# A transformer block on one core: queries and keys by seven block products in place of eight, and the second FFN layer's weights read from DRAM

## The chip, the cores and the metric

The kernel runs on one NeuronCore of a Trainium2 chip. The core has five engines, each with its own queue of instructions, tied to each other by semaphores: TensorE (PE in the profile; its weight loads are a row of their own, PEld), VectorE (DVE), ScalarE (ACT), GpSimd (POOL) and SyncE (SP), which here only issues DMAs. Matmuls write to PSUM, everything else lives in SBUF. The metric is the time of one execution in microseconds. Before the change the median of three runs is 2196.39 us (2195.55 to 2197.65).

## The reference, cut to what matters

A parallel block: layer norm, then attention with rotary embedding and a three-layer FFN side by side, and both are added to x. There are 16 batches of 512 tokens with 256 features, 8 heads of 128, and FFN layers of 1024, 1024 and 256 whose weights are +1 or -1.

```python
xn = _layernorm(x)                                # x: (16, 512, 256) float32
q = rope(einsum('bim,mhd->bhid', xn, wq))
k = rope(einsum('bim,mhd->bhid', xn, wk))
v = einsum('bim,mhd->bhid', xn, wv)
s = einsum('bhid,bhjd->bhij', q, k) / 128 - 1e30 * (i < j)
p = softmax(s)
att = einsum('bhim,hdm->bim', einsum('bhij,bhjd->bhid', p, v), wo)
h = concatenate([xn, -xn])
for kb, s_i in ((k0, s0), (k1, s1), (k2, s2)):    # relu(h) * 2 between layers
    h = s_i * (h @ where(kb, 1.0, -1.0))
out = x + att + h
```

For one head q (128 by 512, features by tokens) is wq's two 128-row blocks times xn's two 128-feature blocks, and k is the same with wk.

## The kernel before, in words

**Slots.** The work is cut in slots, one for each head of each batch: 128 slots, g = 8 b + h. TensorE's order is written out by hand: all code from L580 on runs under a manual schedule for PE. The order on the other engines is chosen by the framework's scheduler, which takes a program's order as priority and puts an instruction where it thinks that its inputs are ready; `behind` (L198) adds an order without a semaphore. A plain slot (`slot`, L547, heads 2 to 7) issues on TensorE: the queries and keys of the next head (`project_qk(g + 1)`), score row 0 of its own head, `ffn2` of the tile two heads back (8 records of 256 columns), row 1, four matmuls of `ffn1`, row 2, four more, row 3, four more, the output projection of head g - 2 (`project_o`), the rest of the `ffn1` tile, and `attend(g - 1)`, the product of v with the transposed probabilities of the slot before. Slots of heads 2 and 7 end with `project_v` (6.9 us of matmuls). Head 0's slot (`slot_of_head_0`) holds the last tile of the batch before and the whole first FFN layer (`ffn0`); head 1's (`slot_of_head_1`) has no `ffn2`, and the output projection stands behind row 0. A matmul with float32 operands shows as two records, one with float32r operands as one.

**Queries and keys.** `project_qk` (L314) makes q and k by two 512-column matmuls each, into one PSUM bank each of a ring of three (`ps_mm`). ACT copies the two halves of the partitions crosswise into `sw` (L326, L327), DVE multiplies the PSUM tile by `cos_sb` (L329), GpSimd multiplies `sw` by `sin_sb` (L330) and adds (L331). The results are qT and kT, wanted by the score rows of the next slot. wq is scaled by 1/128 beforehand (`scale_wq`).

**Probabilities.** `score_row` (L335) is one matmul; DVE adds the causal mask and takes the maximum (L340, L342), ACT the exponential (L345), DVE the reciprocal of the sum, rl (L347), GpSimd the product (L348). Two PSUM banks hold the rows. `turn` (L352) transposes 32 by 32 blocks on DVE into z (L356), and `carry` (L233) moves them to their places in pT by sixteen small DMAs, 40 KB each, from SP's queue. `attend` in the next slot reads pT.

**FFN.** `ffn0` and `ffn1` (L424, L443) split each activation in a high and a low float32r part (ACT makes the high one, DVE the low one). The weights are made once from bytes: `make_w1` makes all of w1, 1024 by 1024, and it stays in SBUF (32 KB of each partition) for all batches.

**The next batch's xn.** `layernorm` (head 3), `transpose_xn` (head 4) and `carry_xn_out` (end of head 5) put it through DRAM; `carry_xn_back` (head 6, one DMA behind each score row, from ACT's queue) brings it to the layout xnT, from which `split_xn` (head 7) makes the FFN's inputs.

Of the kernel before, what the change touches and what calls it, by code (L numbers as in the profile page):

```python
# [11 lines left out]
U8 = mybir.dt.uint8  # L12
# [10 lines left out]
def kernel(  # L23
# [79 lines left out]
    x_first = xpool.tile([P, NT, M], F32, tag="x", name="x_first")  # L103
# [4 lines left out]
    wq_sb = wpool.tile([P, NM, HD], F32, tag="wq", name="wq_sb")  # L108
    wk_sb = wpool.tile([P, NM, HD], F32, tag="wk", name="wk_sb")
# [6 lines left out]

    cos_sb = cpool.tile([P, T], F32, tag="cos", name="cos_sb")
# [4 lines left out]
    k1_sb = work.tile([P, NF0, F1], U8, tag="v", name="k1_sb")  # L122
# [3 lines left out]
    load_w(nc.sync, wq_sb, wq, 0, 2)  # L126
    load_w(nc.scalar, wk_sb, wk, 0, 2)
# [8 lines left out]
    load_w(nc.sync, wq_sb, wq, 2, H)  # L136
    load_w(nc.sync, wk_sb, wk, 2, H)
    nc.sync.dma_start(k1_sb, k1.rearrange("(c p) f -> p c f", p=P))
# [14 lines left out]
    w1_sb = wpool.tile([P, NF0, F1], F32R, tag="w1", name="w1_sb")  # L153
# [26 lines left out]
    def make_w1(reduced, raised):  # L180
        for c in range(NF0):
            if c % 2:
                behind(nc.scalar.activation(
                    w1_sb[:, c, :], k1_sb[:, c, :], AF.Identity,
                    bias=nsg_sb[:, 1:2], scale=sg2_sb[:, 1:2],
                ), raised)
            else:
                behind(nc.vector.tensor_scalar(
                    w1_sb[:, c, :], k1_sb[:, c, :], sg2_sb[:, 1:2], sg_sb[:, 1:2],
                    ALU.mult, ALU.subtract,  # L190
                ), reduced)
# [14 lines left out]
    xns, zxs, bounces, xnTs, halves = {}, {}, {}, {}, {}  # L206

    def layernorm(b, xt, after=None):

        st = small.tile([P, NT, nc.vector.BN_STATS_DIM], F32, tag="st", name=f"st_{b}", bufs=2)  # L210
        mv = small.tile([P, NT, nc.vector.BN_AGGR_DIM], F32, tag="mv", name=f"mv_{b}", bufs=2)
        for c in range(NT):
            begun = nc.vector.bn_stats(st[:, c, :], xt[:, c, :])
            behind(begun, after)
            nc.vector.bn_aggr(mv[:, c, :], st[:, c, :])
        rs = small.tile([P, NT], F32, tag="rs", name=f"rs_{b}", bufs=2)
        nc.gpsimd.tensor_scalar(rs, mv[:, :, 1], LN_EPS, None, ALU.add)
        raised = nc.gpsimd.tensor_tensor(rs, rs, half_sb, ALU.pow)
        xn = npool.tile([P, NT, M], F32, tag="xn", name=f"xn_{b}")
        for c in range(NT):  # L220
            nc.vector.tensor_scalar(
                xn[:, c, :], xt[:, c, :], mv[:, c, 0:1], rs[:, c : c + 1],
                ALU.subtract, ALU.mult,
            )
        xns[b] = xn
        return raised
# [22 lines left out]
    def transpose_xn(b, after):  # L249
        xn = xns.pop(b)  # L250
        zx = work.tile([P, NQ, NM, NT, Q], F32, tag="z", name=f"zx_{b}")
        for c in range(NT):
            behind(nc.vector.transpose(
                zx[:, :, :, c, :].rearrange("p j m a -> p m j a"),
                xn[:, c, :].rearrange("p (m j a) -> p m j a", j=NQ, a=Q),
            ), after)
        zxs[b] = zx
# [36 lines left out]


# [18 lines left out]
    def project_qk(g):  # L314
        b, h = divmod(g, H)
        res = []
        for name, w in (("q", wq_sb), ("k", wk_sb)):
            pq = ps_mm.tile([P, T], F32, tag="mm", name=f"p{name}_{b}_{h}")
            for m in range(NM):
                nc.tensor.matmul(  # L320
                    pq, w[:, m, ts(h, D)], tokens(xnTs[b], m),
                    start=(m == 0), stop=(m == NM - 1),
                )

            sw = work.tile([P, T], F32, tag="sw", name=f"sw{name}_{b}_{h}")
            nc.scalar.copy(sw[0:HALF, :], pq[HALF:D, :])  # L326
            nc.scalar.copy(sw[HALF:D, :], pq[0:HALF, :])  # L327
            rt = work.tile([P, T], F32, tag=f"{name}T", name=f"{name}T_{b}_{h}")
            nc.vector.tensor_tensor(rt, pq, cos_sb, ALU.mult)  # L329
            nc.gpsimd.tensor_tensor(sw, sw, sin_sb, ALU.mult)  # L330
            nc.gpsimd.tensor_tensor(rt, rt, sw, ALU.add)  # L331
            res.append(rt)
        qks[g] = res
# [109 lines left out]
    def ffn1(b, f):  # L443
        ph = ps_mm.tile([P, T], F32, tag="mm", name=f"ph1_{b}_{f}")
        for c in range(NF0):
            for i in range(2):
                nc.tensor.matmul(  # L447
                    ph, w1_sb[:, c, ts(f, P)], h0s[b][i][:, c, :],
                    start=(c == 0 and i == 0), stop=(c == NF0 - 1 and i == 1),
                )  # L450
                if c < NF0 - 1 or i == 0:
                    yield
# [22 lines left out]
    def scale_wq(engine, h0, h1, after):  # L475

        for c in range(NM):
            cols = wq_sb[:, c, h0 * D : h1 * D]
            if engine is nc.scalar:
                behind(engine.mul(cols, cols, 1.0 / D), after)  # L480
            else:
                behind(engine.tensor_scalar(cols, cols, 1.0 / D, None, ALU.mult), after)

    def first_slot():
        l0 = [ffn0(0, f) for f in range(NF0)]
        project_qk(1)
        rest(project_v(0, 0))
        for ic in range(NT):
            reduced, raised = score_row(0, ic)
            rest(l0[ic])  # L490
        turn(0, reduced)
        scale_wq(nc.scalar, 2, H, raised)
        rest(*l0[NT:])
        make_w1(reduced, raised)

    def slot_of_head_0(g):

        b = g // H
        if b < B:
            l0 = [ffn0(b, f) for f in range(NF0)]  # L500
            project_qk(g + 1)
        last = ffn2(b - 1, NF1 - 1)
        if b == B:
# [4 lines left out]
            return  # L508
        for ic in range(NT):
            reduced, _ = score_row(g, ic)  # L510
            if ic == 0:
                rest(ffn2(b - 1, NF1 - 2))
            elif ic == 1:
                rest(ffn1(b - 1, NF1 - 1))
# [10 lines left out]
    def slot_of_head_1(g):  # L525
        b = g // H
        if b < B:
            project_qk(g + 1)
            tile = ffn1(b, 0)
        else:  # L530
            tile = iter(())
        for ic, n in enumerate((0, 4, 3, 3)):
            if b < B:
                reduced, _ = score_row(g, ic)
            if ic == 0 and g > 1:
                project_o(g - 2)
            some(tile, n)
        if g == 1:
            make_w2(reduced)
        if b < B:  # L540
# [6 lines left out]
    def slot(g):  # L547
        b, h = divmod(g, H)
        if g + 1 < N_SLOTS:
            project_qk(g + 1)  # L550
        tile = ffn1(b, h - 1)
        for ic in range(NT):
            reduced, raised = score_row(g, ic)
            if h == H - 2 and b + 1 < B:
                carry_xn_back(b + 1, ic, raised)
            if ic == 0:
                rest(ffn2(b, h - 2))
            else:
                some(tile, 4)
        turn(g, reduced)  # L560
# [4 lines left out]
        attend(g - 1)  # L565
        if h == 2:
            for gv in range(1, HD // (VH * D)):
                rest(project_v(b, gv))
        if b + 1 < B:
            if h == H - 3:  # L570
                carry_xn_out(b + 1, raised)
# [8 lines left out]
    with tc.manual_schedule(engines={mybir.EngineType.PE}):  # L580
        with tc.manual_schedule(engines={mybir.EngineType.DVE}):
            scale_wq(nc.gpsimd, 0, 2, layernorm(0, x_first))
            transpose_first_xn()
            make_scales()
            project_qk(0)
# [57 lines left out]
```

## Time and profile before

| | |
|---|---|
| median of three runs | 2196.39 us |
| the profiled execution | 2196.68 us, of which the span from first to last instruction is 2194.7 |
| granted TensorE clock | 0.999 of full speed |
| matmuls pq and pk (L320) | 512 + 512 records of 128x512 |
| DMA engines | mean 57 GB/s; pT<-z 2048 issues, 1.9 us to landing |
| HBM | 23.33 MB read, 16.25 MB written |

A row of a group of instructions reads: line, engine, operation, out<-in by the program's names, shape and count, busy time, mean duration of one, and the idle time of the engine just before them with what ended it. In a timeline the columns are start and duration in us, engine, line, operation, names and count, and in brackets the idle time before and its releaser. The ends of matmuls are modelled, so the step from one start to the next is what a matmul costs. From batch to batch it is 135.6 us (two slots of head 1 start at 990.25 and 1125.84).

### The profile page before, as it was taken

How to read it: one execution, taken by the hardware profiler on the slowest of the kernel's cores; microseconds unless marked ns; L12 is line 12 of the kernel's file. 1: busy time of each engine (PE TensorE's matmuls, PEld its weight loads, DVE VectorE, ACT ScalarE, POOL GpSimd, SP SyncE). 2: the span in 40 equal slices, each digit the busy share in tenths (PEclk: the TensorE clock that was granted, in tenths of full speed). 3: DMA queues.
4: the chain of work that ended last, by engine and by line, in shares of the span. 5: the costliest groups of instructions: out<-in, count | busy, mean ns of one | idle time of the engine just before them, and what ended most of it. 6: DMA issues, size and time to landing. Idle time of an engine off the chain costs nothing.

```text
span 2194.7 us, 30483 instructions
## 1 busy us (share of the span) xinstructions
PE 2168.8 (99%) x9736; PEld 1548.3 (71%) x9736; DVE 1191.9 (54%) x3005; ACT 867.3 (40%) x1945; POOL 944.6 (43%) x1067
## 2 busy tenths in 40 slices
PE   7999999999999999999999999999999999999998
PEld 3677777777777777776776767777777777777766
DVE  5545655456555565555655555555545655456544
ACT  5344343343434344343343433434334343443432
POOL 4443534435344353434534344353533534435342
PEclk9999999999999999999999999999999999999999
DMA  5122212222121221212211122121221211222111
GB/s 161 41 63 56 61 42 55 59 56 66 43 58 50 57 67 44 60 48 56 67 51 55 49 57 64 52 59 44 56 68 51 60 43 52 66 55 59 43 44 51
DMA packets 134286, 125.55 MB, mean 57 GB/s; under 512 B 37744, under 2 KB 130928, under 8 KB 134128
## 3 DMA queue, kind: packets, MB, share of 16 engines
q1 hardware_dynamic: 122192, 107.09, 18.5%
q10 hardware_dynamic: 11936, 16.52, 2.2%
q8 instruction: 78, 1.28, 0.2%
q14 instruction: 80, 0.66, 0.1%
HBM read 23.33 MB, written 16.25 MB: 18 GB/s over the span
## 4 chain that ended last, share of the span: by engine, by line
PE 97%; SPq 1%; DMA 1%; ACT 1%; DVE 0%; issue 0%; POOL 0%; ACTq 0%; DVEq 0%
PE ph L447 21%; PE y L399 15%; PE po L373 13%; PE s L339 12%; PE pv L307 10%; PE pq L320 10%; PE pk L320 10%; PE ph L432 5%; SPq L237 1%; DMA wk_sb<-in_L_attn_wk_dram 0%; DMA pT<-z 0%; DVE z L356 0%; DMA k_sb<-in_L_ffn_k_dram 0%; POOL swk L330 0%; POOL kT L331 0%
## 5 line engine op out<-in xcount | busy, mean ns | idle before, releaser
L330 POOL TENSOR_TENSOR swq<-swq,sin_sb 128x512 f32<-128x512 f32 x128 | 165.5, 1293 | 959.6 <-ACT swq L327 959.6
L447 PE MATMUL ph<-h0h,w_sb 128*128 128x512 f32 x1024 | 517.9, 506 | 0.0
L345 ACT ACTIVATE p<-s,nmax 128x128 f32<-128x128 f32 (+3 forms) x512 | 270.6, 529 | 380.3 <-DVE nmax L342 329.6
L447 PE MATMUL ph<-h0l,w_sb 128*128 128x512 f32 x1024 | 408.8, 399 | 0.0
L339 PE MATMUL s<-kT,qT 128*128 128x128 f32 (+3 forms) x1024 | 360.5, 434 | 1.9 <-ACT p L345 1.9
L348 POOL TENSOR_SCALAR p<-p,rl 128x128 f32<-128x128 f32 (+3 forms) x512 | 269.7, 537 | 203.9 <-DVE rl L347 202.5
L329 DVE TENSOR_TENSOR qT<-pq,cos_sb 128x512 f32<-128x512 f32 x128 | 88.6, 692 | 462.2 <-ACT swq L327 462.2
L373 PEld LDWEIGHTS po<-pT,v 128*128 128x128 f32 x2560 | 304.7, 192 | 17.4 <-issue 4.4
L373 PE MATMUL po<-pT,v 128*128 128x128 f32 x2560 | 306.9, 275 | 3.7 <-DMA pT<-z 3.1
L356 DVE STREAM_TRANSPOSE z<-p 128x128 f32<-128x128 f32 (+3 forms) x512 | 234.2, 489 | 70.5 <-POOL p L348 64.0
L342 DVE TENSOR_REDUCE nmax<-s 128x1 f32<-128x128 f32 (+3 forms) x512 | 251.4, 491 | 12.7
L339 PEld LDWEIGHTS s<-kT,qT 128*128 128x128 f32 x1024 | 183.6, 189 | 88.8 <-issue 60.8
L447 PEld LDWEIGHTS ph<-h0h,w_sb 128*128 128x128 f32 x1024 | 193.0, 188 | 73.6 <-issue 26.9
L447 PEld LDWEIGHTS ph<-h0l,w_sb 128*128 128x128 f32 x1024 | 193.2, 189 | 72.8 <-issue 26.9
L399 PE MATMUL y<-wo_sb,oT 128*128 128x256 f32 x1024 | 241.8, 379 | 0.8 <-DVE oT L379 0.8
L320 PE MATMUL pq<-xnT,wq_sb 128*128 128x512 f32 x512 | 241.8, 595 | 0.0
L320 PE MATMUL pk<-xnT,wk_sb 128*128 128x512 f32 x512 | 240.7, 592 | 0.5 <-DVE qT L329 0.5
L307 PE MATMUL pv<-wv_sb,xnT 128*128 128x512 f32 x512 | 227.0, 596 | 4.5 <-ACT v L311 4.5
L399 PEld LDWEIGHTS y<-wo_sb,oT 128*128 128x128 f32 x1024 | 192.7, 189 | 30.5 <-DVE oT L379 1.0
L326 ACT COPY swq<-pq 64x512 f32<-64x512 f32 x128 | 74.7, 583 | 321.6 <-PE pq L320 321.6
L340 DVE TENSOR_TENSOR s<-s,causal 128x128 f32<-128x128 f32 x512 | 150.9, 295 | 80.7 <-PE s L339 80.7
L320 PEld LDWEIGHTS pk<-xnT,wk_sb 128*128 128x128 f32 x512 | 97.2, 190 | 123.2 <-issue 121.5
(64 smaller groups left out, 2478.9 us busy)
## 6 DMA issues: line engine op xcount, KB each, us to landing
pT<-z SPq DMA_DIRECT2D x2048, 40.0 KB, 1.9
x<-in_L_attn_x_dram SPq DMA_DIRECT2D x64, 128.0 KB, 2.6
out_dram<-x SPq DMA_DIRECT2D x64, 128.0 KB, 2.2
bounce<-zx ACTq DMA_DIRECT2D x15, 512.0 KB, 2.7
xnT<-bounce ACTq DMA_DIRECT2D x60, 128.0 KB, 2.5
wv_sb<-in_L_attn_wv_dram SPq DMA_DIRECT2D x2, 512.0 KB, 10.0
k_sb<-in_L_ffn_k_dram SPq DMA_DIRECT2D x1, 1024.0 KB, 11.2
wo_sb<-in_L_attn_wo_dram SPq DMA_DIRECT2D x1, 1024.0 KB, 12.4
```

What stands on the lines that cost most here:

```text
L307: nc.tensor.matmul(pv, tokens(xnTs[b], m)[:, c], wv_sb[:, m, ts(g, VH * D)], start=(m == 0), stop=(m == NM - 1),)
L320: nc.tensor.matmul(pq, w[:, m, ts(h, D)], tokens(xnTs[b], m), start=(m == 0), stop=(m == NM - 1),)
L330: nc.gpsimd.tensor_tensor(sw, sw, sin_sb, ALU.mult)
L339: nc.tensor.matmul(ps[:, :n], qT[:, ts(ic, P)], kT[:, :n], start=True, stop=True)
L340: nc.vector.tensor_tensor(ps[:, ts(ic, P)], ps[:, ts(ic, P)], causal, ALU.add)
L342: reduced = nc.vector.tensor_reduce(nmax, ps[:, :n], AX.X, ALU.max, negate=True)
L345: raised = nc.scalar.activation(p, ps[:, :n], AF.Exp, bias=nmax, accum_out=l)
L348: nc.gpsimd.tensor_scalar(p, p, rl, 1.0, ALU.mult, ALU.mult)
L356: behind(nc.vector.transpose(zs[:, :, block(ic, 0) : block(ic + 1, 0), :].rearrange("p j c a -> p c j a"), p.rearrange("p (c j a) -> p c j ...
L373: nc.tensor.matmul(po[:, ts(ic, P)], vt[:, jc, ts(h % VH, D)], pT[:, :, block(ic, jc), :], start=(jc == 0 and ic == 0), stop=(jc == ic), s ...
L399: nc.tensor.matmul(ys[b][c // 2][:, c % 2, :], lhsT[:, ts(c, P)], rhs, start=(y_done[b][c] == 0 and c % 2 == 0), stop=(y_done[b][c] == N_Y ...
L447: nc.tensor.matmul(ph, w1_sb[:, c, ts(f, P)], h0s[b][i][:, c, :], start=(c == 0 and i == 0), stop=(c == NF0 - 1 and i == 1),)
```

## The change

Tokens are split in two halves, 0 to 255 and 256 to 511, and features in two blocks; with them q and k of a head, stacked, are a 2 by 2 block product with 256-column blocks: eight products before, seven by Strassen's scheme now. The seven left factors are made once (`w7_sb`, from wq and wk by scaling and differences, in `make_w7`), the four differences of xn's blocks once a batch (`make_ts`). The factor 1/128 is split, 1/16 for q and 1/8 for k. The products accumulate in two banks, pa and pb; in between ACT copies partial sums out (ca, cb, cu), since they serve q as well as k, and DVE adds them to q and k in SBUF, from which the rotation then reads. The seven products are spread over the slot: four at its start, one behind score row 0, one behind `ffn2` (in head 1's slot: behind the output projection), one before row 2. Heads 0 and 1 of the first batch keep the direct form.

w1 is no longer held whole: a tile of 512 KB for each of its eight column blocks, two in SBUF at a time. In batch 0 the tiles are made from bytes, one a slot, and stored in DRAM; from batch 1 on `load_w1` reads one back at the start of each slot, from SP's queue. Some tiles share other places (xn with xh, zx with xl, x_first with h0h), the xn of the next batch is carried out behind row 0 of head 5 and back behind rows 2 and 3 of head 5 and rows 0 and 1 of head 6, and `make_ts` follows at the end of head 6's slot.

```diff
-    wq_sb = wpool.tile([P, NM, HD], F32, tag="wq", name="wq_sb")
-    wk_sb = wpool.tile([P, NM, HD], F32, tag="wk", name="wk_sb")
+    w7_sb = wpool.tile([P, 7, HD], F32, tag="w7", name="w7_sb")
+    WQ0, WQ1, WK0, S1, S2, WK1, S4 = range(7)
...
+    def load_w1(b, f):
+        if (b, f) == (1, 0):
+            nc.sync.dma_start(w1_dram[NF1 - 1], w1s[0, NF1 - 1].bitcast(F32))
+        if 0 < b < B:
+            w1s[b, f] = wpool.tile([P, NF0, P], F32R, tag="w1", name=f"w1_{b}_{f}", bufs=2)
+            nc.sync.dma_start(w1s[b, f].bitcast(F32), w1_dram[f])
+        elif b == 0:
+            if f:
+                nc.sync.dma_start(w1_dram[f - 1], w1s[0, f - 1].bitcast(F32))
+            if f + 1 < NF1:
+                load_k1(f + 1)
...
+    def make_ts(b, after=None):
+        t = tts[b] = npool.tile([P, 4, NQ // 2, P], F32, tag="tt", name=f"tt_{b}")
+        x11, x12, x21, x22 = (xn_half(b, m, i) for m in range(2) for i in range(2))
+        for out_, a, c in (
+            (0, x12, x11), (2, x22, x12), (1, x22, t[:, 0]), (3, t[:, 1], x21),
+        ):
+            behind(nc.vector.tensor_tensor(t[:, out_], a, c, ALU.subtract), after)
...
+    def rotate(src, name, g, engine):
+        sw = work.tile([P, T], F32, tag="sw", name=f"sw{name}_{g}")
+        nc.scalar.copy(sw[0:HALF, :], src[HALF:D, :])
+        nc.scalar.copy(sw[HALF:D, :], src[0:HALF, :])
+        rt = work.tile([P, T], F32, tag=f"{name}T", name=f"{name}T_{g}")
+        nc.vector.tensor_tensor(rt, src, cos_sb, ALU.mult)
+        engine.tensor_tensor(sw, sw, sin_sb, ALU.mult)
+        engine.tensor_tensor(rt, rt, sw, ALU.add)
+        qks.setdefault(g, []).append(rt)
...
     def project_qk(g):
+        product(pa[:, :n], WQ0, xn_half(b, 0, 0), start=True, stop=False)
+        product(pa[:, n:], WQ1, xn_half(b, 1, 0), start=False, stop=True)
+        ca = work.tile([P, T], F32, tag="ca", name=f"ca_{g}", bufs=1)
+        nc.scalar.copy(ca, pa)
+        product(pb[:, n:], S1, t[:, 0], start=True, stop=False)
+        product(pb[:, :n], WK1, t[:, 3], start=False, stop=True)
+        cb = work.tile([P, T], F32, tag="cb", name=f"cb_{g}", bufs=1)
+        nc.scalar.copy(cb, pb)
+        yield
+        product(pa[:, :n], S2, t[:, 1], start=False, stop=False)
+        cu = work.tile([P, n], F32, tag="cu", name=f"cu_{g}", bufs=1)
+        nc.scalar.copy(cu, pa[:, :n])
+        yield
+        product(pb[:, n:], S4, xn_half(b, 1, 1), start=False, stop=True)
+        q = work.tile([P, T], F32, tag="qk", name=f"q_{g}")
+        nc.vector.tensor_tensor(q[:, :n], ca[:, :n], ca[:, n:], ALU.add)
+        nc.vector.tensor_tensor(q[:, n:], cu, pb[:, n:], ALU.add)
+        rotate(q, "q", g, nc.gpsimd)
+        yield
+        product(pa[:, :n], WK0, t[:, 2], start=False, stop=True)
+        k = work.tile([P, T], F32, tag="qk", name=f"k_{g}")
+        nc.vector.tensor_tensor(
+            k.rearrange("p (i t) -> p i t", i=2),
+            pa[:, :n].unsqueeze(1).broadcast_to([P, 2, n]),
+            cb.rearrange("p (i t) -> p i t", i=2), ALU.add,
+        )
+        rotate(k, "k", g, nc.gpsimd)
+        yield
...
     def slot(g):
         b, h = divmod(g, H)
-        if g + 1 < N_SLOTS:
-            project_qk(g + 1)
+        load_w1(b, h)
+        qk = project_qk(g + 1) if g + 1 < N_SLOTS else iter(())
         tile = ffn1(b, h - 1)
+        some(qk, 1)
         for ic in range(NT):
             reduced, raised = score_row(g, ic)
...
             if ic == 0:
+                some(qk, 1)
                 rest(ffn2(b, h - 2))
+                some(qk, 1)
             else:
                 some(tile, 4)
+            if ic == 1:
+                rest(qk)
         turn(g, reduced)
...
+        if b == 0:
+            make_w1(h, reduced, raised)
+        if g == 2:
+            make_w7(0, 2, reduced, raised, True)
...
+            if h == H - 2:
+                make_ts(b + 1, reduced)
```

`make_w7` is called in the first slots; for two of the heads at a time it is four scalings on ACT and four differences on DVE:

```diff
+        for place, scale in (
+            (WK1, -K_SCALE), (WK0, K_SCALE), (WQ0, Q_SCALE), (WQ1, Q_SCALE)
+        ):
+            if not scaled:
+                behind(nc.scalar.mul(w[place], w[place], scale), raised)
...
+        for out_, a, c in ((S1, WK0, WK1), (S2, S1, WQ0), (S4, WQ1, S2), (WK0, WQ0, WK0)):
+            behind(nc.vector.tensor_tensor(w[out_], w[a], w[c], ALU.subtract), reduced)
```

## The prediction

> **What bounds the kernel now.** I read the page first: busy shares, then the chain of work that ended last, then the list of waits.
>
> ```profile
> span 2194.7 us, 30483 instructions
> PE 2168.8 (99%) x9736; PEld 1548.3 (71%) x9736; DVE 1191.9 (54%) x3005; ACT 867.3 (40%) x1945; POOL 944.6 (43%) x1067
> ...
> PE 97%; SPq 1%; DMA 1%; ACT 1%; DVE 0%; issue 0%; POOL 0%; ACTq 0%; DVEq 0%
> ```
>
> TensorE is busy all along, and the chain lies on it for 97%. So what is taken out of TensorE's queue comes off the span, until another chain is late. Which one is next is read from one plain slot in the timeline (head 4 of batch 8; columns: start, length, engine, line, operation):
>
> ```profile
> 1174.48 1.88 PE L320 MATMUL pq<-xnT,wq_sb 128*128 128x512 f32 x4
> 1176.20 1.88 PE L320 MATMUL pk<-xnT,wk_sb 128*128 128x512 f32 x4
> 1177.92 0.38 PE L339 MATMUL s<-kT,qT 128*128 128x128 f32 x2
> ...
> 1186.43 2.39 PE L373 MATMUL po<-pT,v 128*128 128x128 f32 x20
> 1188.66 1.88 PE L320 MATMUL pq<-xnT,wq_sb 128*128 128x512 f32 x4
> ```
>
> A slot is 14.18 us from pq to pq; attend's po begins at 11.95 of it. That po reads the pT of the slot before, and what carries pT there is the second chain: score row 3, exponential, GpSimd's product with rl, DVE's transpose z, sixteen DMAs from SP's queue. GpSimd in this slot:
>
> ```profile
> 1177.73 1.29 POOL L330 TENSOR_TENSOR swq<-swq,sin_sb 128x512 f32<-128x512 f32 x1 [2.13 <-ACT swq L327]
> ...
> 1181.70 1.27 POOL L331 TENSOR_TENSOR kT<-kT,swk 128x512 f32<-128x512 f32 x1
> 1183.07 1.40 POOL L348 TENSOR_SCALAR p<-p,rl 128x128 f32<-128x128 f32 x3
> 1185.25 0.70 POOL L348 TENSOR_SCALAR p<-p,rl 128x512 f32<-128x512 f32 x1 [0.79 <-DVE rl L347]
> ```
>
> It works without a break from 3.25 to 9.99, then waits 0.79 us for rl: row 3's product ends at 11.47 and GpSimd is not what holds it. Now the tightest handover, from head 1 to head 2 (three lines of DVE, SP and PE; the slot of head 1 starts at 1125.84, the next at 1139.23):
>
> ```profile
> 1138.49 0.70 DVE L356 STREAM_TRANSPOSE z<-p 128x512 f32<-128x512 f32 x1
> ...
> 1139.26 10.14 SPq L237 DMA_DIRECT2D pT<-z  x16
> ...
> 1151.18 1.05 PE L373 MATMUL po<-pT,v 128*128 128x128 f32 x8
> ```
>
> Sixteen issues take 10.14 us, the last (0.6 long) lands 1.9 us after its start (the page's DMA list): 11.4 us from first issue to all landed, at 1150.7. po starts at 1151.18: **0.5 us of room**. In the plain slot z ends at 12.26, pT has landed at 12.3 + 11.4 = 23.7, po wants it at 14.18 + 11.98 = 26.16: 2.4 us of room.
>
> **What the change takes off TensorE.** A 512-column f32 record costs (1177.92 - 1174.48)/8 = 0.43 us. The nearest row for 256 columns is the output projection:
>
> ```profile
> 1183.56 1.71 PEld L399 LDWEIGHTS y<-wo_sb,oT 128*128 128x128 f32 x8
> ```
>
> Eight weight loads, one for each record of 256 columns, in 1.71 us: 0.215 each, so a load (0.19) still hides. Eight records of 0.43 (3.44) become fourteen of 0.215 (3.01): 0.43 us a head, for the 126 heads that use the scheme **54 us**, 3.4 us a batch. The plain slot becomes 13.75 us and po moves from 11.95 to 11.52 in it.
>
> **What it adds on TensorE's own path.** S2's product waits for ACT's copy ca, S4's for cb, WK0's for cu. By the row of v<-pv a 512-column copy is 0.59 us and ACT starts 0.26 us after the product ends. pa is done at 0.86 of the slot, ca at 1.71; TensorE reaches S2 at 1.94 (four products 1.72, score row 0 0.22). Cost 0, behind score row 0; without that cover it is the 0.26 + 0.59 us of the copy, less what lies between. S4 comes after the second layer's tile of ffn2 (0.95 us) and WK0 after four more records: both free. cu is 256 columns, some 0.37 us. The bounds for all three are 0 and 0.3 us a slot; I take 0.
>
> **What it adds elsewhere.** DVE: two sums of 256 (0.42 each by the 128x256 rows) and one of 512 (0.69): 1.5 us a head, and make_ts 1.7 a batch, to 64% of its time. ACT: 1.55 us a head, to 48%. Neither is a bound. But the heads' rotation starts later, because q exists only after S4 and k only after WK0. In the plain slot S4 ends at 1.72 + 0.22 + 0.43 + 0.95 + 0.43 = 3.75; DVE's sum takes it to 4.4, ACT's two swap copies (0.58 each) to 5.65, so GpSimd begins swq at 5.7 in place of 3.25. From there its queue has no gap: four products at 1.29, rows 1 to 3 of p at 0.49, 0.59, 0.70: 6.9 us, **ending at 12.6 in place of 11.47**. Row 3 of p, which pT's carry waits for, is last in that queue.
>
> **A rule that speaks against the change.** The start of the trace has DVE operations with two SBUF inputs beside GpSimd ones:
>
> ```profile
> 18.23 1.38 DVE L289 SCALAR_TENSOR_TENSOR xl<-xnT,c_sb,xh 128x1024 fp32r<-128x1024 f32 x1 [0.49 <-ACT xh L286]
> ...
> 18.49 2.24 POOL L330 TENSOR_TENSOR swk<-swk,sin_sb 128x512 f32<-128x512 f32 x1
> ...
> 19.53 4.48 DVE L176 SCALAR_TENSOR_TENSOR w_sb<-k_sb,sg_sb,kb 128x1024 fp32r<-128x1024 uint8 x2
> ...
> 20.81 2.12 POOL L331 TENSOR_TENSOR kT<-kT,swk 128x512 f32<-128x512 f32 x1
> ...
> 25.11 1.26 POOL L330 TENSOR_TENSOR swk<-swk,sin_sb 128x512 f32<-128x512 f32 x1
> ```
>
> GpSimd's product, 1.26 us alone, takes 2.24 beside xl and ends 1.12 us after xl's end (19.61): while xl ran it hardly moved. kT ends (22.93) 1.12 us after the first w_sb (21.81): again one at a time, and w_sb too waited its turn. [...] Before the change the rotation's first product reads pq from PSUM and meets no lock (its 0.69 us stands beside GpSimd in every slot). After it, src is the SBUF tile q or k: q's and k's cosine products and q's first sum now lock, and make_ts four times a batch. q's product (4.6 to 5.3) falls where GpSimd is idle, k's (0.69, near 7) into its full queue. By durations alone row 3 of p ends at 12.6; by the rule at 13.2. The start-up rows bear it out, so I take 13.2.
>
> **pT is then late.** z adds 0.75: first issue near 13.95, landed at 25.35, and po wants it at 13.75 + 11.52 = 25.3. By the rule plain slots sit on the edge (0 to 0.1); by durations alone they keep 0.6. A stall at po lengthens its own slot and so spares the next. By handover and batch:
>
> - Head 1 to 2: the output projection (1.73) stands where a plain slot has ffn2 (0.95), so all is 0.75 later: GpSimd ends near 13.8, issue at 14.6, landed at 26.0; po wants 25.34 - 0.86 = 24.5. **Stall 1.5.**
> - Head 3 to 4: 0.1; head 4 to 5: 0.2 with the carry of xn moved into it.
> - Heads 5 to 6 and 6 to 7 together: make_ts puts four subtractions (4 x 0.42) where DVE waits for row 3. That the scheduler fills this gap is seen in the plain slot, where two zx transposes sit in it. They take turns with GpSimd at the lock, and z ends near 15.2: landed at 26.7 against 25.3, 1.4; the copies of xn, which made these two landings about 1 us later than others in this profile, add some 0.5. **Stall 1.9.**
> - Heads 7, 0 and 2 hand over across 7 us or more of other matmuls: 0.
>
> Sum 3.7 us a batch against 3.4 gained; 16 batches: +5 us.
>
> **The stream of w1.** One 512 KB load on SP's queue a slot from batch 1 on. bounce<-zx is the row: same size, 2.7 us to landing, 0.34 us to issue. SP issues 10 of 14 us, and its wait (the tile two back, read by TensorE before attend) is over before z is ready, so nothing queues behind it; the tile is used 5 us into the next slot. Cost 0, cover about 8 us; the bound is that its packets hold up pT's, at most its 2.7 us in a carry. In batch 0 make_w1, make_w7 and make_ts sit on DVE and ACT at slots' ends: make_w7's four scalings and four differences ahead of make_ts, less the old make_w1 (four at 0.84 on DVE, four at 1.24 on ACT, all in slot 0). 0 to 12 us, I take 7. The earlier carry of xn costs nothing: ACT waits for its landing 5 us after an issue that needs 2.7.
>
> **Sum** on the profiled execution's own 2196.7 us (span 2194.7; the median of the runs is 2196.4, the same within their spread): 2196.7 - 54 + 59 + 7 = **2209**, own range 2193 to 2235.
>
> **Rivals.**
> 1. *TensorE's gain stays* (faster, chance 0.32). The lock is seldom met, z goes ahead of make_ts; plain slots keep their 0.6 us, only head 2 stalls, 1.2 us, and head 7 by 0.3: 2196.7 - 54 + 24 + 5 = 2172. For it: 2.4 us of room in plain slots now. Against: the start-up rows.
> 2. *The streams stretch the carry* (slower, 0.15): w1's packets among pT's sixteen make each carry 1.2 us longer. As stalls alternate, three more of 1.2 a batch: 3.6 x 16 = 58 more, 2267. For: head 5's landings are 1 us late beside xn's copies. Against: x's four loads of 128 KB just ahead of head 2's carry leave it at some 10 us.
> 3. *TensorE waits for ca in every slot* (slower, 0.10): it decides once ACT ends ca later than 1.94; at 0.3 us, 126 x 0.3 = 38 more: 2247. For: a margin of only 0.2 us. Against: ACT is idle there (3.37 us before swq in plain slots).
>
> The forecast has 0.43. **Range 2158 to 2265**: from rival 1 without any stall but head 2's to rival 2. Within 0.2% (2192 to 2201, about what a measurement of this kernel can tell from no change) lies a part of the forecast, 0.09; faster 0.33, slower 0.58.
>
> **What would show it.** Products of 0.215 us a record, 3.0 us a head; GpSimd's row 3 of p straight behind other work, with no wait for rl; some of its 1.29 us products at about 2; idle time before po, released by pT's DMA, of about 60 us in place of 3.1, most of it in the slots of heads 2, 6 and 7. No idle time before po and a time near 2150 would refute the second chain; idle before S2 on ca would mean rival 3, landings late by a microsecond after an issue on time rival 2.

## The result and the profile after

| | before | after |
|---|---|---|
| median of the runs | 2196.18 us (5 runs) | 2312.79 us (5 runs) |
| profiled execution | 2196.7 us, span 2194.7 | 2308.7 us, span 2306.9 |
| mean granted TensorE clock | 0.999 | 0.989 |
| TensorE's idle time (span less busy) | 25.9 us | 142.9 us |

The change makes the kernel slower: 1.0525 of the time before (95% interval 1.0508 to 1.0542), 117 us more by the medians, where the forecast had 12 (2209 - 2196.7). The page's lines that answer to the first ones shown of before (the span; busy time; the chain that ended last):

```profile
span 2306.9 us, 33246 instructions
PE 2164.0 (94%) x10492; PEld 1705.9 (74%) x10492; DVE 1438.6 (62%) x3463; ACT 1077.2 (47%) x2332; POOL 986.5 (43%) x1063
...
PE 54%; SPq 14%; POOL 13%; issue 7%; DVE 7%; DMA 4%; ACT 2%; POOLq 0%; ACTq 0%; DVEq 0%
```

Before, 97% of the chain lay on TensorE. Now nearly half of it runs through the other engines and SP's queue: GpSimd, DVE and the sixteen issues of pT's carry. That is the second chain of the prediction. The list of TensorE's waits has it by name (us in total, times, longest):

```profile
PE po L460 <- DMA pT<-z: 70.6, 38, 3.5
PE s L426 <- ACT p L432: 41.4, 44, 1.9
```

The first line was foreseen, at 60 us. The second was not.

The place of the loss is best seen slot by slot. From the trace, the mean time from score row 0 of one head to score row 0 of the next, and TensorE's idle time in it (batches 3 to 14; for before only head 2 has any, 0.08):

| slot of head | 0 | 1 | 2 | 3 | 4 | 5 | 6 | 7 |
|---|---|---|---|---|---|---|---|---|
| before | 22.73 | 13.39 | 21.19 | 14.20 | 14.19 | 14.20 | 14.21 | 21.06 |
| after | 22.30 | 12.85 | 24.89 | 13.78 | 16.52 | 16.86 | 14.02 | 21.48 |
| idle after | 0 | 0 | 2.58 | 0 | 2.22 | 2.34 | 0.13 | 0.60 |

Heads 0, 1 and 3 show the gain undisturbed: 0.42 to 0.54 us. Heads 2, 4 and 5 give it all back, and the three lose 8.7 us a batch. Head 2 loses 1.1 us more than its idle time explains (24.89 - 21.19 = 3.70, against 2.58). Counting the 0.43 us that each slot should have gained, TensorE's own work grew by 1.6 us in head 2's slot and by 0.5 and 0.75 in those of heads 4 and 5. For head 2 the clock, shown below, is most of it; the other two were not traced.

**The handover from head 1 to head 2**, batch 8 again; lines of the timeline of the changed kernel (this slot begins at 1175.22, and TensorE's line is the one that reads this pT, a slot later):

```profile
1186.76 1.27 POOL L359 TENSOR_TENSOR kT<-kT,swk 128x512 f32<-128x512 f32 x1
1188.01 0.59 POOL L435 TENSOR_SCALAR p<-p,rl 128x384 f32<-128x384 f32 x1
1188.63 0.58 DVE L443 STREAM_TRANSPOSE z<-p 128x384 f32<-128x384 f32 x1 [2.50 <-POOL p L435]
1189.13 0.12 DVE L434 RECIPROCAL rl<-l 128x1 f32<-128x1 f32 x1
...
1189.35 0.70 POOL L435 TENSOR_SCALAR p<-p,rl 128x512 f32<-128x512 f32 x1 [0.75 <-DVE rl L434]
1190.08 0.71 DVE L443 STREAM_TRANSPOSE z<-p 128x512 f32<-128x512 f32 x1 [0.24 <-POOL p L435]
...
1190.82 10.76 SPq L260 DMA_DIRECT2D pT<-z  x16
...
1203.28 4.10 PE L460 MATMUL po<-pT,v 128*128 128x128 f32 x20 [3.26 <-issue]
```

Read it from the third line. DVE stands 2.50 us before the transpose of row 2, because GpSimd makes row 2's product only after kT. The reciprocal rl of row 3 is queued on DVE behind that transpose, though ACT had been done with row 3 at 1186.10 and DVE stood idle from 1186.13 on. So GpSimd, done with row 2 at 1188.60, waits 0.75 us for an rl that DVE could have made some 3 us earlier. A closed circle: GpSimd (row 2) holds DVE, DVE (rl) holds GpSimd (row 3). The first issue comes at 15.6 of the slot where the forecast had 14.6, and po stalls 3.26 us instead of 1.5. (The profile names no releaser for this one wait; the last of the sixteen DMAs lands at 1202.9, and po starts 0.4 us later.)

The order on DVE is not new. In the static order of the instructions, row 2's transpose stands ahead of row 3's rl in 111 of 128 slots before the change and in 96 after it. Before, row 2's product was long done when DVE came to it. The group tells it (last columns: mean ns of one; idle time ahead of the group), first before, then after:

```profile
L356 DVE STREAM_TRANSPOSE z<-p 128x384 f32<-128x384 f32 x128 | 69.6, 544 | 2.8 <-POOL p L348 2.7
```

```profile
L443 DVE STREAM_TRANSPOSE z<-p 128x384 f32<-128x384 f32 x128 | 73.6, 575 | 246.5 <-POOL p L435 246.5
L435 POOL TENSOR_SCALAR p<-p,rl 128x512 f32<-128x512 f32 x128 | 89.4, 698 | 92.1 <-DVE rl L434 92.1
```

2.8 us of waiting have become 246.5: in the mean of batches 3 to 14, 2.5 us in each slot of heads 1 to 5 and 7. None of this is TensorE's time; it is a delay that DVE passes on, to pT by way of rl and to all else that stands behind the transpose in its queue.

**After the wait, po itself is slower.** 20 records of po took 4.10 us above, against 2.39 in the plain slot of before. The view by windows gives the granted clock (the number after POOL's): first that po, then the po of the slot before it, which had not waited.

```profile
1203.28:1207.21 3.93, 3.93 (x20) 3.93 (x21) 0.81 (x2) 0.00 (x0) 0.00 (x0) 0.57 0.39 118
1185.84:1187.99 2.15, 2.15 (x21) 2.15 (x20) 0.29 (x1) 0.85 (x3) 2.07 (x2) 1.00 0.30 107
```

The clock is 0.57 and the time nearly double (3.93 us against 2.15). Over the run the group po is busy for 329.9 us, before for 306.9: 23 us more, nearly all of it in ten slots of head 2 and three others.

**The slot of head 4** has the waits of the second kind. DVE's queue at its start (row 0 of the scores is done by TensorE at 1229.8), and TensorE:

```profile
1231.68 0.74 DVE L244 TENSOR_SCALAR xn<-x,mv,rs 128x256 f32<-128x256 f32 x2 [1.48 <-POOL rs L241]
...
1233.91 0.29 DVE L427 TENSOR_TENSOR s<-s,causal 128x128 f32<-128x128 f32 x1
...
1235.13 0.91 PE L426 MATMUL s<-kT,qT 128*128 128x384 f32 x2 [1.56 <-ACT p L432]
...
1237.60 1.12 PE L426 MATMUL s<-kT,qT 128*128 128x512 f32 x2 [0.63 <-ACT p L432]
```

The layernorm of the next batch stands ahead of row 0's mask: DVE waits 1.48 us for GpSimd's rs, makes xn, and comes to the mask 4.1 us after the scores were there. In the mean of batches 3 to 14 this mask starts 4.3 us after the start of score row 0; before the change it was 0.4. The layernorm itself comes late because its first operation on DVE (1227.07) stands behind the late transpose and rl of head 3. The two PSUM banks of s are then both taken, and rows 2 and 3 wait for ACT's exponentials: 2.2 us in the slot of head 4, and head 4's pT is late as well, which head 5's slot pays (1.7 of its 2.3 us of idle time are before po).

### The profile page after: what moved, and what is told of

Same layout as the page of the kernel before. It is cut to its first block, busy times and chain, and to the rows that moved or that the text cites. A ratio compares the mean times of both kernels' runs of the same rounds, so it can differ in the third digit from the quotient of the medians.

```text
span 2306.9 us, 33246 instructions
## 1 busy us (share of the span) xinstructions
PE 2164.0 (94%) x10492; PEld 1705.9 (74%) x10492; DVE 1438.6 (62%) x3463; ACT 1077.2 (47%) x2332; POOL 986.5 (43%) x1063
## 3 DMA queue, kind: packets, MB, share of 16 engines
q10 hardware_dynamic: 11936, 16.52, 2.2%
## 4 chain that ended last, share of the span: by engine, by line
PE 54%; SPq 14%; POOL 13%; issue 7%; DVE 7%; DMA 4%; ACT 2%; POOLq 0%; ACTq 0%; DVEq 0%
SPq L260 14%; PE po L460 10%; PE pv L344 9%; PE ph L534 8%; PE y L486 7%; PE pa L388 5%; PE ph L519 5%; PE s L426 5%; PE pb L388 4%; DMA pT<-z 4%; POOL p L435 3%; POOL kT L359 2%; POOL swk L358 2%; POOL swq L358 2%; DVE z L443 2%
## 5 line engine op out<-in xcount | busy, mean ns | idle before, releaser
L534 PE MATMUL ph<-h0h,w 128*128 128x512 f32 x1024 | 521.0, 509 | 0.0
L534 PE MATMUL ph<-h0l,w 128*128 128x512 f32 x1024 | 409.8, 400 | 0.0
L460 PE MATMUL po<-pT,v 128*128 128x128 f32 x2560 | 329.9, 287 | 79.9 <-DMA pT<-z 70.6
L426 PE MATMUL s<-kT,qT 128*128 128x128 f32 (+3 forms) x1024 | 365.7, 439 | 41.5 <-ACT p L432 41.4
L534 PEld LDWEIGHTS ph<-h0l,w 128*128 128x128 f32 x1024 | 194.0, 189 | 72.5 <-issue 26.8
L534 PEld LDWEIGHTS ph<-h0h,w 128*128 128x128 f32 x1024 | 193.6, 189 | 72.2 <-issue 26.9
L348 ACT COPY v<-pv 128x512 f32<-128x512 f32 x128 | 74.9, 586 | 280.4 <-PE pv L344 280.3
L359 POOL TENSOR_TENSOR qT<-qT,swq 128x512 f32<-128x512 f32 x127 | 199.8, 1573 | 10.0
L408 DVE TENSOR_TENSOR q<-ca 128x256 f32<-128x256 f32 x126 | 52.6, 417 | 233.1 <-ACT ca L396 232.9
L396 ACT COPY ca<-pa 128x512 f32<-128x512 f32 x126 | 73.8, 586 | 245.4 <-PE pa L388 245.4
L344 PEld LDWEIGHTS pv<-wv_sb,xnT 128*128 128x128 f32 x512 | 96.6, 194 | 109.2 <-issue 105.0
L359 POOL TENSOR_TENSOR kT<-kT,swk 128x512 f32<-128x512 f32 x127 | 163.6, 1288 | 9.9
```

Of the source, the lines that this page charges most:

```text
L344: nc.tensor.matmul(pv, tokens(xnTs[b], m)[:, c], wv_sb[:, m, ts(g, VH * D)], start=(m == 0), stop=(m == NM - 1),)
L359: engine.tensor_tensor(rt, rt, sw, ALU.add)
L426: nc.tensor.matmul(ps[:, :n], qT[:, ts(ic, P)], kT[:, :n], start=True, stop=True)
L460: nc.tensor.matmul(po[:, ts(ic, P)], vt[:, jc, ts(h % VH, D)], pT[:, :, block(ic, jc), :], start=(jc == 0 and ic == 0), stop=(jc == ic), s ...
L534: nc.tensor.matmul(ph, w1s[b, f][:, c], h0s[b][i][:, c, :], start=(c == 0 and i == 0), stop=(c == NF0 - 1 and i == 1),)
```

## The experiments

Each kernel was run beside the kernel before on the same chip (medians of before: 2197.3, 2194.1 and 2195.5 us in three groups); ratios are to it, with the 95% interval.

**1. rl ahead of row 2's transpose.** In score_row and turn:

```
-        nc.vector.reciprocal(rl, l)
+        rls[g] = nc.vector.reciprocal(rl, l)
...
-            ), after)
+            ), rls[g] if ic == 2 else after)
```

> Only DVE's order changes: the transpose of row 2 of p stands behind row 3's reciprocal, in every slot. Theory (the wait of that transpose for GpSimd holds up rl, and so row 3's product by some 0.75 us in the tight handovers): GpSimd's wait before row 3's product (92.1 us in all at 128x512) falls below 30, three to four stalls a batch shrink by some 0.7: 2308 - 35 to 50 = 2258 to 2273. Rival (GpSimd's own queue ends last, as the forecast had it): rl comes earlier but row 3's product does not start earlier; within 10 us of 2308.

Measured: 2270.9 us, 1.0345 (1.0330 to 1.0360), 42 us less than the changed kernel. GpSimd's group for row 3:

```profile
L436 POOL TENSOR_SCALAR p<-p,rl 128x512 f32<-128x512 f32 x128 | 88.9, 695 | 20.7 <-DVE rl L435 20.7
L444 DVE STREAM_TRANSPOSE z<-p 128x384 f32<-128x384 f32 x128 | 73.6, 575 | 219.4 <-POOL p L436 219.4
```

The wait for rl fell from 92.1 to 20.7. DVE still waits 219 us for row 2. That no longer holds rl, but it still holds what else stands behind it: row 0's mask of head 4 starts 3.7 us after score row 0, against 4.3 in the changed kernel. The circle was a cause, and worth about a third of the loss (42 of 117 us).

**2. GpSimd's kT behind row 3's product** (on top of experiment 1). The last product of k's rotation is emitted after score row 3 and tied behind row 3's product:

```
+        if late:
+            return lambda after: behind(engine.tensor_tensor(rt, rt, sw, ALU.add), after)
         engine.tensor_tensor(rt, rt, sw, ALU.add)
...
+        finish.pop(g + 1)(scaled[g])
         turn(g, reduced)
```

> The kernel with rl ahead of the second transpose, and besides GpSimd's last rotation product (kT of the next head, 1.29 us) stands behind row 3's product instead of ahead of row 2's. Theory (with rl in time GpSimd's own queue sets row 3's product, as the forecast had it): row 3's product comes up to 1.3 us earlier, the stalls in the slots of heads 2, 4, 5 (2.1, 1.6, 2.0 us) shrink by about 1 us each and more where po then runs at full clock: 2271 - 50 to 75 = 2196 to 2221. Rival (kT is then late for the next slot's row 0): TensorE waits for POOL's kT and the time stays above 2250.

Measured: 2185.6 us, 0.9955 (0.9941 to 0.9970): 85 us off, more than expected, and faster than before the change. The same two groups:

```profile
L439 POOL TENSOR_SCALAR p<-p,rl 128x512 f32<-128x512 f32 x128 | 89.5, 699 | 22.0 <-DVE rl L438 22.0
L447 DVE STREAM_TRANSPOSE z<-p 128x384 f32<-128x384 f32 x128 | 73.6, 575 | 89.4 <-POOL p L439 89.4
```

TensorE waits for kT once, 0.5 us; in head 3's slot kT now ends at 11.2 us after score row 0 instead of 10.1, and the next score row comes at 13.8. Idle time in the slots of heads 2, 4 and 5 fell from 2.06, 1.55, 1.97 to 0.75, 0.44, 0.90. Between the two profiled executions, whose spans are 90 us apart, 64 are TensorE's idle time (117.8 to 54.2) and 26 its busy time (2156.3 to 2129.8): with the long waits the slow po went too. The step did more than the expectation counted: it takes 1.29 us out from ahead of row 3's product, and it also gives DVE row 2 earlier, so that DVE's wait fell from 219 to 89 us, row 0's mask of head 4 from 3.7 to 2.3 us and the waits of s from 25.0 to 6.6 us. How the 85 us divide between the two was not tried.

**3. The lock, by itself and with rl in time.** The prediction's lock is that GpSimd and a DVE operation with two operands in SBUF take turns, as its start-up rows show (GpSimd's product 2.24 us in place of 1.26). q and k are summed in place in PSUM, so that the cosine product has one operand in SBUF:

```
-        q = work.tile([P, T], F32, tag="qk", name=f"q_{g}")
+        q = pb
...
-        k = work.tile([P, T], F32, tag="qk", name=f"k_{g}")
+        k = pa
```

> q and k are summed in place in their PSUM banks, not into SBUF tiles, so the cosine products have one operand in SBUF only. k's sum is two of 256 columns in place of one of 512. Theory (the two engines take turns where both of DVE's inputs are in SBUF): DVE's kT falls from 1.09 us to 0.7, GpSimd's qT from 1.57 to 1.29; 0.3 us off the chain to pT in four handovers a batch: 2308 - 20 = 2288, unless PSUM banks held longer make TensorE wait. Rival (the lock is the main loss): 2250 or less.

> Both together: rl ahead of the second transpose, and q and k left in PSUM. Theory (the lock lies on GpSimd's queue, which sets row 3's product only once rl is in time): now its 0.3 to 0.5 us a slot count, 2271 - 15 to 40 = 2231 to 2256. Rival (the lock is hidden in any order): within 8 us of 2271.

The groups of the changed kernel, then with q and k in PSUM:

```profile
L357 DVE TENSOR_TENSOR kT<-k,cos_sb 128x512 f32<-128x512 f32 x126 | 137.3, 1089 | 0.5
L359 POOL TENSOR_TENSOR qT<-qT,swq 128x512 f32<-128x512 f32 x127 | 199.8, 1573 | 10.0
```

```profile
L357 DVE TENSOR_TENSOR kT<-pa,cos_sb 128x512 f32<-128x512 f32 x126 | 87.0, 690 | 38.5 <-ACT swk L355 33.9
L359 POOL TENSOR_TENSOR qT<-qT,swq 128x512 f32<-128x512 f32 x127 | 163.4, 1287 | 9.9
```

With both of DVE's operands in SBUF, DVE's product takes 0.40 us longer (1.09 against 0.69) and GpSimd's, beside it, 0.29 (1.57 against 1.29). (Operands in SBUF alone do not cost it: q's product, at a time when GpSimd is idle or has 0.06 us left, takes 0.68 us in the changed kernel.) Removing it alone gave 2309.4 us, 1.0525 (1.0504 to 1.0546): nothing, where 20 us were expected. GpSimd's wait for rl of row 3 grew from 92.1 to 101.3 us, head 2's slot by 0.5 us, and the waits of the product pb for make_ts from 2.0 to 5.9 us. With rl in time it gave 2250.0 us, 1.0245 (1.0231 to 1.0259), 21 us less than experiment 1: the number expected, but not by the way expected. In head 3's slot row 3's product ends no earlier (11.4 us after score row 0 in both); it ends 0.5 to 1.0 us earlier in the slots of heads 2, 4 and 5, in which row 0's mask had been late (1.6, 3.7 and 1.1 us after the start of its score row, against 0.4). The edit also takes DVE time away and splits k's sum, so the 21 us are the price of the edit. The lock is real, and a small part.

**4. The layernorm out of row 0's way.** The four xn products move from the end of head 3's slot behind row 0's reduce in head 4's slot:

```
+                if h == H - 4 and b + 1 < B:
+                    normalise(b + 1, reduced)
```

> The changed kernel, with the four products xn of the layernorm moved from the end of head 3's slot behind row 0's reduce of head 4's slot, so that DVE does not stand waiting for GpSimd's rs ahead of row 0's mask. Theory (row 0's mask comes late in head 4's slot, so score rows 2 and 3 wait for a PSUM bank and the whole chain to pT of head 4 is late): the waits of s for ACT fall from 41 us to under 15, the slots of heads 4 and 5 (16.5 and 16.9 us) lose 1 to 1.5 us each: 2308 - 32 to 48 = 2260 to 2276. Rival (GpSimd's queue alone sets pT there): the waits of s go, the one at po grows by as much: above 2295.

Measured: 2283.8 us, 1.0401 (1.0374 to 1.0429): 29 us less, just short of the expected. The waits of s fell from 41.4 to 8.4 us, head 4's slot from 16.5 to 15.1; head 5's only from 16.9 to 16.4. The pT that it reads still stands in the circle: row 3's product in head 4's slot waits 0.75 us for rl.

**5. No reload of w1.** Two blocks of the second layer stay in SBUF and serve for all, so this kernel leaves the other blocks' weights out and shows only a time:

```
+            if (b, f) >= (1, 2):
+                w1s[b, f] = w1s[1, f % 2]
+                return
```

> Leaves out the reload of the second layer's weights from batch 1's third block on: two blocks stay in SBUF and are used for all. Theory (pT is late through the engines, not through the DMA): within 10 us of 2308. Rival (the stream's packets or its place in SP's queue stretch pT's carry): the stalls before po shrink by 1 us each, 50 us or more less, below 2260.

Measured: 2311.6 us, 1.0530 (1.0508 to 1.0552). Nothing changed, the slots neither (head 2's 24.6, head 4's 16.5, head 5's 16.8). The rival that the stream stretches pT's carry falls.

**6. attend later.** If pT's lateness is the loss, giving it five more microseconds must end it. attend of a head moves behind score row 2 of the slot after the next:

```
             else:
+                if ic == 2:
+                    attend(g - 2)
                 some(tile, 4)
...
         rest(tile)
-        attend(g - 1)
```

> attend of a head moves from the end of the next slot to behind score row 2 of the slot after that, so pT has some 5 us more. Nothing else changes. Theory (pT late): TensorE's idle time before po, 79.9 us in the changed kernel, falls below 5; the mean granted clock returns from 0.989 to 0.997 or more, worth some 20 us; the waits of s for ACT (41) stay. Time near 2308 - 75 - 20 = 2213, between 2195 and 2230. Rival (TensorE is held by something else, the stream of w1 or waits of the products): the idle time turns up before other instructions and the time stays above 2270.

Measured: 2181.4 us, 0.9932 (0.9917 to 0.9947), lower than the expected 2195 to 2230. TensorE does not wait before po at all, po takes 2.12 us between first and last record in all 128 slots, the mean clock is 0.997. The waits of s went as well (7.5 us), which was not expected: oT's copy no longer stands ahead of row 0's mask there, but whether that is the reason was not tried. In place of both are two smaller ones:

```profile
PE pb L388 <- DVE tt L330: 12.1, 18, 1.6
...
PE s L426 <- ACT p L432: 7.5, 11, 0.7
```

**7. The same later attend in the kernel before.** The edit is that of experiment 6.

> The kernel before with attend behind score row 2 of the slot after the next, and nothing of the change. It says what the later attend is worth by itself. Theory (before the change pT was not late, 3.1 us in all): within 6 us of 2197, so that the 16 us by which the first experiment's kernel beats the one before are the scheme's. Rival (the later attend is a gain in itself, and the scheme only a loss): 2182 or less.

Measured: 2224.4 us, 1.0132 (1.0115 to 1.0149). Both theories missed: the later attend is a loss of 30 us there (before in the same group: 2194.1). Head 4's slot grows from 14.19 to 15.75 with 1.29 us of idle time, and s waits for ACT (19.9 us). So with the same placing of attend, the scheme and the stream together are worth 2224.4 - 2181.4 = 43 us, where the prediction took 54 off TensorE. It is not a pure measure of the scheme: each of the two kernels keeps stalls of its own in the slots of heads 4 and 6, 1.6 and 1.3 us a batch.

**8. Matmuls in the wait.** The value projections at the ends of the slots of heads 2 and 7 go ahead of attend:

```
         rest(tile)
+        if h == 2:
+            for gv in range(1, HD // (VH * D)):
+                rest(project_v(b, gv))
...
         attend(g - 1)
```

> The changed kernel with the value projections at the ends of the slots of heads 2 and 7 put ahead of attend instead of behind it: 3.4 us of matmuls that TensorE has to do anyway stand between it and pT. No other order changes. Theory (TensorE waits for pT[...]): head 2's slot falls from 24.9 to 20.7 - 21.3 us, which is its idle time of 2.6 and the 1.7 that po is longer; head 7's by 0.8; the mean clock rises to 0.992 or more; 2308 - 65 to 80 = 2228 to 2243. Rival (the wait only moves to the next handover): head 3's slot grows from 13.8, the time stays above 2270.

Measured: 2277.9 us, 1.0380 (1.0364 to 1.0396), 35 us less where 65 to 80 were expected. Head 2's slot fell by 3.0 us, to 21.86, and the clock rose to 0.995. The wait before po in it is gone, but a new one stands in the middle of the projection:

```profile
PE pv L344 <- DVE h1l L543: 31.3, 31, 1.3
```

The projection takes a PSUM bank that DVE's h1l frees, and h1l is late in the same DVE queue, behind the transposes of rows 2 and 3. Head 7's slot even grew, from 21.5 to 22.2. The expectation had counted the matmuls and not the bank. Its 1.5 us for a slow po is an estimate that the changed kernel's trace does not bear out: the seven waits of 1.50 to 1.80 us before po left it at its 2.19 us from first to last record, and the shortest wait with a slow po is 1.87.

**9. Faster versions.** Experiment 6 with the layernorm's xn at the end of head 4's slot and make_ts behind row 2's reduce in head 6's slot:

> The first experiment's kernel (attend late) with two more moves: the layernorm's xn products go to the end of head 4's slot, and the four subtractions of make_ts behind row 2's reduce in head 6's slot instead of row 3's. Theory: the slots of heads 4 and 6 lose the 0.95 and 0.7 us by which they are longer than a plain one: 2181 - 26 = 2155, between 2148 and 2168. Rival: DVE's added work only moves to the next slot: 2175 to 2182.

Measured: 2168.3 us, 0.9878 (0.9863 to 0.9893), the fastest of all: 13 us less than experiment 6, where 26 were expected. Heads 4 and 6 came to 13.79 as expected, and more than half of that turned up in heads 5 and 7 (14.53 and 21.29), where y waits for a late h1l.

Two more, with xn made by ACT (`nc.scalar.activation(..., AF.Identity, bias=nb, scale=rs)`) and make_ts in another order, on experiment 2 and on experiment 6:

> The kernel with kT last (2185.6), with the layernorm's xn products moved from DVE to ACT behind row 0 of head 4's slot (scale rs, bias minus mean times rs, the latter by two small GpSimd operations), and make_ts in the order 0, 1, 3, 2. Theory (head 4's slot loses the wait of s and with it pT of head 4 comes in time): the slots of heads 4 and 5 (14.5 and 15.05) come to 13.8 - 14.2: 2185 - 20 to 30 = 2155 to 2165. Rival: within 6 us of 2185.

> The kernel with attend late (2181.4) with the same move of xn to ACT and the same order of make_ts, and without the two moves of the tuned one. Theory: heads 4, 5 and 6 lose 0.95, 0.28 and 0.5 to 0.9 us: 2181 - 28 to 34 = 2147 to 2153. Rival: ACT's four products delay row 1's or row 2's exponential and s waits again: 2165 or more.

Measured: 2176.1 us, 0.9915 (0.9902 to 0.9929), and 2180.7 us, 0.9935 (0.9923 to 0.9948). The first took head 4's slot from 14.49 to 14.01 and left head 5's at 15.01, so what is left of head 5's stall is not the layernorm's: 10 us instead of 20 to 30. The second missed: head 4 came to 14.00, but head 5's slot rose to 14.69 with y waiting for h1l, and head 6 stayed at 14.7.

## Why the prediction was wrong, step by step

- **TensorE's gain** (0.43 us a head, 54 us): right. Undisturbed slots gained 0.42 to 0.54, and experiments 6 and 7 differ by 43 us.
- **Waits for ca, cb, cu** taken as 0: right. None is in the list of the changed kernel.
- **GpSimd's row 3 of p "straight behind other work, with no wait for rl", and DVE no bound at 64% of its time**: this is the step that failed. DVE's share came out as forecast (62%), but DVE now stands 2.5 us in six of eight slots ahead of row 2's transpose, whose product GpSimd makes behind kT, and what its order puts behind that transpose is late: rl of row 3, and in head 3's slot the layernorm. Row 3's product ended at 13.86 in a plain slot (head 3 of batch 8), after a wait of 0.75 us for rl; without the wait it would have ended at 13.1, where the forecast had 13.2. So GpSimd's own queue was worked out right, and the prediction did not ask what stands ahead of rl on DVE. The wait for row 2 of p had been 2.8 us in the whole run, so the row gave no warning; only the order of DVE's instructions did. Experiment 1 prices rl at 42 us, experiment 4 the layernorm at 29.
- **The lock**, 0.6 to 0.7 us on row 3 (13.2 for 12.6): right in kind, half the size. It was an estimate from the start-up rows, and no run shows this term by itself; what the runs show in its place is 0.29 us on qT and 0.40 on DVE's kT. q's first sum, counted in as well, was never beside a GpSimd operation: 0.42 us, as the second (0.41). make_ts meets it as foreseen: at 273.7 its first two subtractions take 1.06 and 1.51 us beside GpSimd's products, the other two 0.40 and 0.38. The edit that takes it off q's and k's products is worth 0 alone and 21 us once rl is in time.
- **Heads 3 to 4 and 4 to 5, 0.1 and 0.2 us of stall**: wrong by 2 us each, and by slot length 2.7 and 2.9 us a batch, the largest part of what the forecast lacked. Head 4's slot stalls at s, 2.2 us, since the layernorm and oT's copy stand ahead of row 0's mask; experiment 4 took 33 us of the s waits away and 29 us of time. The prediction followed DVE only at the end of a slot. Head 5's stall has three sources: head 4's pT is made in that late slot, with the circle on top, and its carry is slow.
- **"The earlier carry of xn costs nothing"**: wrong by about 1 us. Head 4's pT lands 12.7 us after its first issue, those of the other heads after 11.5 to 11.9 (means of batches 3 to 14); before the change it was head 5's that came late, 12.3. The lateness has moved with xn's DMAs: in batch 8 the last three issues of head 4's carry take 2.9 to 3.4 us to land, beside two DMAs xnT<-bounce, and those just ahead of them 1.9. It stays in experiment 2 (12.8 against 11.5 to 11.7 for most others), where this lateness of some 1.1 us is more than head 5's idle time of 0.90; without the reload of w1 it is 12.4. No run moved xn's DMAs back, so the cause is read from the traces and not tried.
- **Head 1 to 2, 1.5 us**: 2.58 in the mean. The issue came 1.0 us later, 0.75 of it the wait for rl. The carry, 10.8 us long in the slot shown, was 10.2 in the mean, as forecast.
- **make_ts in heads 6 and 7, 1.9 us**: too much; 0.13 and 0.60 of idle time, 1.1 together by slot length.
- **A stall priced by its length**: too little. In 13 of the long ones the granted clock over po was 0.50 to 0.69: 23 us more.
- **The stream of w1, 0, and the start, 7 us**: the first is right (experiment 5). Score row 0 of batch 1 comes at 159.5 us, before at 159.9: with some 3.4 us gained in eight slots, the start costs at most about 3, since batch 0 has stalls too.

The rival of TensorE's gain kept (2172) comes near what experiments 2, 6 and 9 reach with other orders; in this kernel its reasons (plain slots keep 0.6 us of room, the lock is seldom met) did not hold. The sign of the forecast was right, but it was the balance of 54 us gained and 66 lost, and could have fallen either way; its size lacked DVE's lateness (the circle and head 4's slot), the slow carry and the clock. The stated range did not follow from its own sums (without head 7's stall rival 1 is 2167, and rival 2's 2267 lies outside it), but the measured 2313 is far beyond either. Experiments 1 and 4 (42 and 29 us) overlap with each other and with the 23 of the clock, so they are not a sum. What remains in head 2's slot in experiment 2 (0.75 us of idle) was not traced further, and streaming w1 in the kernel before, without the scheme, was not tried.

## What to carry to other kernels

When work is pushed later on one engine, look in the static order of every engine that it feeds for an instruction that stands ahead of something urgent: an order that cost 3 us for as long as its input was early can cost forty when it is late. A saving on the busiest engine is safe only if the handover that comes next keeps its room; here one cure was not to make the chain faster but to take its result up a slot later (experiment 6), within 4 us of the cure by order (experiment 2). The same step cost the kernel before 30 us (experiment 7), so it is for a handover that is late. And a stall on TensorE can cost more than its length: in 13 slots of the changed kernel with 1.87 to 3.52 us of it, po then took 0.9 to 2.1 us longer at a granted clock of 0.50 to 0.69.

## What the runs showed of the hardware

TensorE's granted clock fell after some short waits and not after others. Of the 47 slots of the changed kernel in which po waited for more than 0.3 us, the 24 with less than 1.8 us ran po at its usual pace (2.19 us from first to last record, 2.12 without a wait). Of the 23 with 1.8 to 3.6 us, po took 0.9 to 2.1 us longer in 13 (3.0 to 4.2 us) and no longer in 10 (2.19); the shortest wait with a slow po was 1.87 us, the longest with a full-speed one 3.35.

What tells the two apart in this trace is where the wait falls. The granted clock in it is full or half (1.00 or 0.50), and it is half in thirteen stretches of 3.41 us, one of 6.83 and a last one that the end cuts off; they begin at multiples of 3.413 us from one another: those at 350.19 and 404.80 are 16 such steps apart, those at 350.19 and 1203.52 250. The run can be cut into pieces at these steps. Two pairs of neighbouring pieces, the first number behind the comma being TensorE's busy time and the third from the end the clock:

```profile
1200.11:1203.52 3.41, 0.24 (x2) 0.28 (x3) 1.34 (x4) 0.60 (x1) 1.91 (x3) 1.00 0.33 93
1203.52:1206.94 3.42, 3.42 (x18) 3.42 (x18) 0.57 (x1) 0.00 (x0) 0.00 (x0) 0.50 0.40 120
```

```profile
203.42:206.83 3.41, 1.57 (x8) 0.98 (x6) 0.91 (x4) 0.89 (x3) 2.72 (x3) 1.00 0.23 60
206.83:210.24 3.41, 1.90 (x17) 1.93 (x18) 1.33 (x3) 0.00 (x0) 0.69 (x1) 1.00 0.50 151
```

The wait of 3.26 us in batch 8 lies in one piece, which is idle for 3.17 us, and the next piece has half the clock. The wait of 3.35 us in batch 1 is divided into 1.84 and 1.51 us, and the clock stays full, in the piece behind as well. Counted over the changed kernel's trace, from 40 us on to the last matmuls and where the clock was full: after a piece with 1.99 to 3.17 us of idle time the clock was half in 12 of 12 cases, with 1.78 to 1.90 in 2 of 6 (1.87 and 1.90, but not 1.88), with 1.74 or less in none of 629. In the kernel before no such piece was idle for more than 1.47 us, and the clock stayed full in all of them. In the changed kernel the clock was half for 51 us up to the last matmuls, which costs up to 26 us.
